# Segment attention on one core: TensorE's nine-armed lists become one list with short conditional blocks

## The chip, the cores and the metric

The kernel runs on one core of a Trainium2 chip. The metric is the device time of one execution in microseconds. The kernel before was run eight times: the median is 377.73 us, the lowest 371.74, the highest 382.41.

## The reference

Each of 16384 rows carries a segment number from 0 to 7. Each row gets a place inside its segment, at most 3072 places long, and attention runs among the rows of one segment; the result is projected, normalised over all rows, and added to the input.

```python
q = feat @ Wq; k = feat @ Wk; v = feat @ Wv            # feat 16384x256, q and k 32 wide, v 256 wide
starts = jnp.searchsorted(bids, jnp.arange(B))         # bids is not sorted here
pos = jnp.arange(N) - starts[bids]
qp, kp, vp = (pad(q), pad(k), pad(v))                  # scattered to (8, 3072, .) at [bids, pos]
scores = jnp.where(mask[:, None, :], jnp.einsum('bld,bmd->blm', qp, kp), NEG)
rp = jnp.einsum('blm,bmd->bld', jax.nn.softmax(scores, axis=-1), vp)
t = rp[bids, pos] @ Wt
tn = (t - t.mean(axis=0)) / jnp.sqrt(t.var(axis=0) + EPS) * gamma + beta
return feat + jax.nn.relu(tn)
```

Most rows fall outside the 3072 places and read an edge row, so that a segment really has some hundreds of rows of its own. A tile is 128 such rows. The kernel always handles at least four tiles of a segment and at most six.

## The kernel before, in words

**How the program is made.** The kernel is written as one list of operations in program order (`Program.op`), each with an engine, its reads and its writes. From these `settle` works out which earlier operations it must wait for; `run` then writes one instruction stream for each engine, in list order. An operation that somebody waits for raises its engine's semaphore by one. The position of a line in the source is thus its position in that engine's queue.

**The stages.** The prologue (about 0 to 30 us in the profile) finds the segments' starts, makes the list of rows of segments 0 and 1 and folds Wv and Wt into `wvt`. Then comes a loop over the eight segments, `for e in range(NB)`, here called regions 0 to 7 (about 30 to 278 us). Last, the statistics of the normalisation are finished, and sixteen groups of 1024 rows are loaded, get their edge rows added and are stored, while the segments' own rows go out by GpSimd's scatters (about 278 us to the end).

**A region.** Region e computes attention for segment e and prepares segment n = e + 1. `step(e, u)` with `attend` multiplies the probabilities of query tile u (`pa` for tiles 0 to 3, `pb` for 4 and 5) with the values `vs` of all key tiles into one of two banks `ps_o`; VectorE takes the reciprocal of the denominator (`rdens`), and the row is scaled into `tk`, on ScalarE for odd u and on VectorE for even u. Between the six steps stand, for segment n, transposes of the gathered rows (`xt_main`, `xt_rest`, copied by ScalarE into `xT`), projections (`project`), values (`values`) and scores (`scores`, with exponentials on ScalarE), and for segment e + 2 the list of rows (`own_of`, `prefix`, `list_ahead`, `list_part`, whose last act is to issue gathers on GpSimd). The banks `ps_m` are handed out in turn by `nb()`. `past` puts two VectorE sums per finished tile (`moments`) and a square on ScalarE in the gaps, and `slot` takes the next piece from the list `work` (places, edges, row numbers).

**Absent tiles.** A segment of four tiles has no products with tiles 4 and 5. Before, the whole of region e is written for TensorE nine times, once for each pair of sizes (three sizes of e by three of n); these are the arms. `sizes` computes the arm's number on VectorE, `load` (line 1070) reads it into a TensorE register, and a switch (line 776) jumps to the arm. Region 7 has three arms. Inside an arm there is no branch; at its end stands a jump over the other arms. Only TensorE has arms: the other engines do the work of six tiles always.

**Conditional blocks elsewhere.** In the last part VectorE scales tiles 4 and 5 of each segment inside `v.If(...)` (line 1902), and GpSimd scatters them inside `x.If(...)` (line 1982).

**The order of transfers.** SyncE's queue stores each segment's `tk` rows into `t_rows` (tiles 0 to 3 after step 3, tiles 4 and 5 after step 5), fetches the edge lists `eb`, and in region 7 starts to load the groups `f` (`load_group`, ten buffers, which lie partly over the attention's buffers). These loads stand in SyncE's queue behind the two stores of segment 6.

**The end.** `look` gives each engine a hint for its last branch (line 2006), by which the kernel either ends or runs the general version; TensorE's stands after its last product.

Of the kernel before, what the change touches and what calls it, by code (L numbers as in the profile page):

```python
# [20 lines left out]
P = 128  # L21
# [509 lines left out]
class Op:  # L531
    __slots__ = (
        "n", "eng", "emit", "dma", "region", "pred", "seq", "waits", "needed", "bit", "val",
        "know", "cond", "slot", "loose",
# [3 lines left out]
class Program:  # L538
# [3 lines left out]
    def __init__(self, nc):  # L542
        self.nc = nc
        self.ops = []
        self.count = {e: 0 for e in ENGINES}
        self.rings = {q: {"turn": 0, "held": [None] * n} for q, n in RINGS.items()}
        self.known = {e: ({}, 0) for e in ENGINES}
        self.records = {}
        self.where = {}
        self.region = None  # L550
        self.dmas = 0
# [35 lines left out]
    def op(self, eng, emit, reads=(), writes=(), dma=False, pred=None, cond=None, after=(), loose=False):  # L587
# [4 lines left out]
        o.needed, o.bit, o.val, o.slot = False, None, 0, None  # L592
        o.loose = loose
# [31 lines left out]
    def settle(self, o, deps):  # L625
# [42 lines left out]
        if o.region is None:  # L668
            waits, self.known[eng] = through(self.known[eng])
            o.waits = {None: waits}  # L670
            o.know = self.known[eng]
        else:
            reg = o.region
            o.waits = {}
            for arm in reg["arms"]:
                if o.pred is None or o.pred(arm):
                    o.waits[arm], reg["known"][arm] = through(reg["known"][arm])
            o.know = self.meet(list(reg["known"].values()))
        for waits in o.waits.values():
            for d in waits:  # L680
                d.needed = True
# [17 lines left out]
    def arms(self, reg, arms):  # L699
        assert self.region is None  # L700
        self.region = {"arms": list(arms), "reg": reg, "known": {a: self.known["PE"] for a in arms}}

    def end_arms(self):
        self.known["PE"] = self.meet(list(self.region["known"].values()))
        self.region = None

    def run(self):
        nc = self.nc
        sems = {e: nc.alloc_semaphore(f"at_{e}") for e in ENGINES}
        total = {e: 0 for e in ENGINES}  # L710
        for o in self.ops:
            if not o.dma:
                total[o.eng] += 1 if o.needed else 0
                o.val = total[o.eng]
        rings = {
# [13 lines left out]
        def emit(e, o, waits, inc):  # L729
            for d in waits:  # L730
# [11 lines left out]
            elif inc:  # L742
                i.then_inc(sems[o.eng], inc)

        def stream(eng):
            ops = [o for o in self.ops if o.eng == eng]

            def go(e):
                k = 0
                while k < len(ops):  # L750
                    o = ops[k]
                    if o.region is None:
                        emit(e, o, o.waits[None], 1 if o.needed else 0)
                        k += 1
                        continue
                    reg = o.region
                    end = k
                    while end < len(ops) and ops[end].region is reg:
                        end += 1
                    part = ops[k:end]  # L760
                    arms = reg["arms"]

                    def one(arm):
                        todo = []
                        for x in part:
                            if x.pred is None or x.pred(arm):
                                todo.append([x, 1 if x.needed else 0])
                            elif x.needed:
                                todo[-1][1] += 1
                        for x, inc in todo:  # L770
                            emit(e, x, x.waits[arm], inc)

                    if len(arms) == 1:
                        one(arms[0])
                    else:
                        for a in e.Switch(reg["reg"](e), len(arms)):
                            one(arms[a])
                    k = end

            return go  # L780

        for eng, e in (
            ("SP", nc.sync), ("ACT", nc.scalar), ("DVE", nc.vector), ("PE", nc.tensor), ("POOL", nc.gpsimd)
        ):
            stream(eng)(e)
# [114 lines left out]
def fast_path(nc, feat, bids, wq, wk, wv, wt, gamma, beta, out, bad):  # L900
# [86 lines left out]
    armf, arm = new("armf", [1, NB]), new("arm", [1, 2 * NB], I32)  # L987
    upto, order = new("upto", [1, NB + 1], I32), new("order", [1, NG], I32)
    tiles_i = new("tiles_i", [1, NB], I32)
# [76 lines left out]
    regs = {}  # L1066

    def load(eng, key, ap, hi, lo=0):
# [3 lines left out]
        pg.op(eng, emit, [ap], [])  # L1072
# [123 lines left out]
    def transposes(e, h, tiles, bank_, at0, which):  # L1196
        for t in tiles:
            pred = None if t < 4 or which is None else (lambda a, t=t: a[which] > t - 4)
            pg.tr(
                bank_[:, at0 + (t - tiles[0]) * P : at0 + (t - tiles[0] + 1) * P],  # L1200
                xs[:, e * FT + t, h * P : (h + 1) * P], ident[:], pred=pred,
# [5 lines left out]
    def xt_main(e, h):  # L1207
        b = nb()
        transposes(e, h, range(4), b, 0, None)
        into_xT(h, 0, QA, b[:])  # L1210

    def xt_rest(e, which):
        b = nb()
        for h in range(DH):
            transposes(e, h, range(4, 6), b, h * QB, which)
# [3 lines left out]
    def project(e, c, which, b=None):  # L1219

        b = nb() if b is None else b
        for n, pred in ((QA, None),) if c == 0 else (
            (P, lambda a: a[which] == 1), (QB, lambda a: a[which] == 2)
        ):
            for h in range(DH):
                pg.mm(
                    b[:, 0:n], w4[:, h, :], xT[:, h, c * QA : c * QA + n],
                    start=(h == 0), stop=(h == DH - 1), pred=pred,
                )
# [8 lines left out]
    def values(e, c, which):  # L1238
        b = nb()
        for i in range(2):  # L1240
            t = 2 * c + i
            pred = None if t < 4 else (lambda a, t=t: a[which] > t - 4)
            for h in range(DH):
                pg.mm(
                    b[:, i * D : (i + 1) * D], xT[:, h, t * P : (t + 1) * P], wvt[:, h, :],
                    start=(h == 0), stop=(h == DH - 1), pred=pred,
# [3 lines left out]
    def scores(e, c, tiles, which):  # L1250
        qe, ke = q[e % 2], k[e % 2]
        dst, n = (pa, QA) if c == 0 else (pb, QB)
        kinds = [(n, None)] if c == 0 else [(P, lambda a: a[which] == 1), (QB, lambda a: a[which] == 2)]
        for w, pred in kinds:
            for t in tiles:
                g = slice(32 * (t % 4), 32 * (t % 4) + 32)
                p = pred
                if t >= 4 and c == 0:
                    p = lambda a, t=t: a[which] > t - 4
                elif t == 5 and w == P:  # L1260
                    continue
                pg.mm(ps_s[t % 4][:, 0:w], ke[g, t // 4, :], qe[g, c * QA : c * QA + w], pred=p)
# [4 lines left out]
    def attend(e, u, which, between=None):  # L1267
        po = ps_o[u % 2]
        src, w = (pa, u) if u < 4 else (pb, u - 4)
        for t in (0, 1, 2, 4, 5, 3):  # L1270
            if t == 1 and between is not None:
                between()
            least = max(t, u)
            pred = None if least < 4 else (lambda a, least=least: a[which] > least - 4)
            pg.mm(
                po[:, 0 : D + 1], src[:, t, w * P : (w + 1) * P], vs[e % 2][:, t, :],
                start=(t == 0), stop=(t == 3), pred=pred,
# [3 lines left out]
        if u % 2 or e == NB - 1:  # L1281
            pg.act(tk[:, m, :], po[:, 0:D], AF.Identity, scale=rdens[:, m : m + 1])
        else:
            pg.ts(tk[:, m, :], po[:, 0:D], rdens[:, m : m + 1], ALU.mult)
        if u in (3, 5):
# [24 lines left out]
    def sizes(lo, hi):  # L1310

        n = slice(lo, hi)
        pg.ts(armf[:, n], n_bc[0:1, n], 4.0 * P, ALU.is_ge)
        pg.stt(armf[:, n], n_bc[0:1, n], 5.0 * P, armf[:, n], ALU.is_ge, ALU.add)
        pg.stt(
            arm[:, lo - 1 : hi - 1], armf[:, lo - 1 : hi - 1], 3.0, armf[:, n], ALU.mult, ALU.add,
        )

# [17 lines left out]
    list_ahead(0)  # L1336
# [709 lines left out]
```

## Time and profile before

| | |
|---|---|
| profiled execution, device time | 376.97 us |
| span of its instructions | 372.5 us |
| median of eight runs | 377.73 us |
| TensorE matmul busy | 267.8 us (72%), 1405 records |
| VectorE, ScalarE, GpSimd busy | 236.5, 149.9, 173.9 us |
| regions start on TensorE at | 30.5, 65.2, 92.3, 129.9, 169.4, 201.8, 233.7, 256.3 us |
| instruction fetches of queue q8 | 35 packets, 0.57 MB |

The span runs from the first to the last instruction; the time outside it is 4.5 us in this execution. A float32 product of 128 columns by 256 shows as two matmul records of about 0.22 us from start to start, so that one step of four key tiles has 8 records and one of six tiles has 12. From the records of the steps (8, 8, 10, 12, 12, 12, 8, 8) the segments of this input have 4, 4, 5, 6, 6, 6, 4 and 4 tiles. In the page's second part the span is cut into 40 slices of 9.3 us.

### The profile page before, as it was taken

The numbers are of one execution on the slowest core, as the hardware profiler recorded it, in microseconds if no ns is written. First come the engines' busy times: TensorE is split into PE (matmuls) and PEld (weight loads), VectorE is DVE, ScalarE is ACT, GpSimd is POOL, SyncE is SP. The second block draws the span as 40 slices with busy tenths as digits, with TensorE's granted clock in tenths as the row PEclk, the third lists the DMA queues.
The fourth block names the chain that finished last, engine by engine and source line by source line (L and its number), as shares of the span: only waits on it lengthen the run. The fifth ranks groups of instructions, "written<-read, shape, count | busy, mean of one in ns | idle before, by whom it ended". The sixth has DMA issues, their size and how long they took to land.

```text
span 372.5 us, 4981 instructions
## 1 busy us (share of the span) xinstructions
PE 267.8 (72%) x1405; PEld 177.4 (48%) x1405; DVE 236.5 (63%) x762; ACT 149.9 (40%) x291; POOL 173.9 (47%) x178
## 2 busy tenths in 40 slices
PE   5795883967789599958999897877595895454400
PEld 2563552735556377736776576645362332212100
DVE  5841687694259337722695878346457999999602
ACT  2233856835157336432663726458341131110000
POOL 6506044047726603741278457730603066887770
PEclk9567898996979879998999989898698696855555
DMA  3102013013005110410031022004998989998962
GB/s 90 49 0 60 2 40 116 4 45 101 6 15 160 23 45 24 121 37 18 6 101 35 0 54 82 16 1 154 423 398 362 418 298 425 423 421 334 349 228 114
DMA packets 22497, 52.12 MB, mean 140 GB/s; under 512 B 7503, under 2 KB 15777, under 8 KB 18475
## 3 DMA queue, kind: packets, MB, share of 16 engines
q1 hardware_dynamic: 15610, 40.85, 28.6%
q0 software_dynamic: 6288, 10.01, 8.8%
q8 instruction: 35, 0.57, 0.7%
q10 hardware_dynamic: 544, 0.52, 0.4%
q14 instruction: 20, 0.16, 0.1%
HBM read 25.37 MB, written 28.74 MB: 145 GB/s over the span
## 4 chain that ended last, share of the span: by engine, by line
PE 39%; DVE 32%; issue 12%; ACT 6%; another core or an unknown queue 6%; POOL 2%; POOLq 0%; DVEq 0%
PE ps L801 36%; DVE f L820 7%; DVE tk L820 5%; PE ps L806 3%; DVE acc L840 3%; DVE junk L827 2%; ACT pa L811 2%; DVE k L817 2%; ACT xT L811 1%; POOL sel L829 1%; DVE tk L1903 1%; DVE tk L1905 1%; DVE tk L829 1%; DVE own L840 1%
## 5 line engine op out<-in xcount | busy, mean ns | idle before, releaser
L876 POOL DMA_INDIRECT xs<-in_r_feat,idx x48 | 51.7, 1077 | 108.1 <-DVE idx L840 50.2
L801 PE MATMUL ps<-vs,pa 128*128 128x257 f32 x312 | 87.5, 433 | 17.6 <-issue 13.9
L801 PEld LDWEIGHTS ps<-vs,pa 128*128 128x128 f32 x312 | 65.4, 217 | 34.3 <-issue 18.6
L876 POOL DMA_INDIRECT reads_r<-reads_of,idx x48 | 51.3, 1069 | 14.6 <-issue 14.3
L853 DVE RECIPROCAL rdens<-ps 128x1 f32<-128x1 f32 x48 | 7.8, 162 | 67.2 <-PE ps L801 56.2
L801 PE MATMUL ps<-wvt,xT 128*128 128x256 f32 x156 | 42.9, 423 | 9.6 <-issue 4.7
L892 POOL DMA_INDIRECT out<-tk,idx x32 | 37.5, 1173 | 25.5 <-DVE f L820 14.0
L801 PEld LDWEIGHTS ps<-wvt,xT 128*128 128x128 f32 x156 | 31.5, 208 | 21.1 <-issue 8.4
L801 PE MATMUL ps<-y,hot 16*128 16x256 bf16 x384 | 20.4, 360 | 24.7 <-DVE f L820 21.1
L820 DVE TENSOR_TENSOR f<-f,ps 128x1024 f32<-128x1024 f32 (+3 forms) x17 | 26.2, 1561 | 15.8 <-remote 12.5
L816 ACT COPY f<-ps 128x1024 f32<-128x1024 f32 (+1 forms) x12 | 9.9, 834 | 62.1 <-PE ps L801 47.4
L811 ACT ACTIVATE tk<-ps,rdens 128x256 f32<-128x256 f32 x27 | 12.9, 477 | 51.8 <-DVE rdens L853 40.1
L801 PEld LDWEIGHTS ps<-y,hot 16*128 16x128 bf16 x384 | 11.1, 117 | 42.1 <-DVE f L820 30.6
L811 ACT ACTIVATE pa<-ps,mask 128x512 f32<-128x512 f32 x48 | 29.6, 693 | 3.1 <-PE ps L801 1.4
L811 ACT ACTIVATE xT<-ps,negx 128x512 f32<-128x512 f32 (+1 forms) x32 | 17.1, 586 | 31.7 <-PE ps L806 23.4
L817 DVE COPY k<-ps 32x128 f32<-32x128 f32 x48 | 14.1, 294 | 21.7 <-PE ps L801 11.2
L801 PE MATMUL ps<-f,ident 128*128 128x512 f32 x38 | 25.6, 797 | 1.8 <-DVE ecat L820 1.0
L811 ACT ACTIVATE q<-ps,cqk 96x512 f32<-96x512 f32 (+3 forms) x32 | 18.3, 573 | 17.3 <-PE ps L801 16.3
L801 PE MATMUL ps<-xT,w 128*128 128x512 f32 (+2 forms) x48 | 22.3, 592 | 2.6 <-ACT xT L811 2.6
L840 DVE SCALAR_TENSOR_TENSOR acc<-tk,reads_r,acc 128x256 f32<-128x256 f32 x45 | 21.5, 477 | 2.0 <-issue 1.9
L840 DVE SCALAR_TENSOR_TENSOR acc<-sq,reads_r,acc 128x256 f32<-128x256 f32 x45 | 21.6, 480 | 0.6 <-ACT sq L811 0.6
L801 PE MATMUL ps<-q,k 32*128 32x512 f32 (+2 forms) x124 | 20.5, 555 | 1.3 <-ACT pb L811 1.3
(262 smaller groups left out, 419.2 us busy)
## 6 DMA issues: line engine op xcount, KB each, us to landing
f<-in_r_feat SPq DMA_DIRECT2D x16, 1024.0 KB, 9.8
out<-f SPq DMA_DIRECT2D x15, 1024.0 KB, 6.1
t_rows<-tk SPq DMA_DIRECT2D x8, 512.0 KB
t_rows<-tk SPq DMA_DIRECT2D x8, 256.0 KB, 2.2
eb<-edge_of SPq DMA_DIRECT2D x64, 8.0 KB, 1.4
out<-f SPq DMA_DIRECT2D x2, 512.0 KB, 3.1
xs<-in_r_feat,idx POOLq DMA_INDIRECT x48
reads_r<-reads_of,idx POOLq DMA_INDIRECT x48
```

The costliest lines, as they stand in the source:

```text
L801: "PE", lambda e: e.matmul(out, lhsT, rhs, start=start, stop=stop, skip_group_check=True),
L806: return self.op("PE", lambda e: e.transpose(out, in_, ident), [in_, ident], [out], pred=pred)
L811: "ACT", lambda e: e.activation(out, in_, func, bias=bias, scale=scale), [in_, *more], [out]
L816: return self.op("ACT", lambda e: e.copy(out, in_), [in_], [out])
L817: return self.op(eng, lambda e: e.tensor_copy(out, in_), [in_], [out])
L820: return self.op(eng, lambda e: e.tensor_tensor(out, a, b, op), [a, b], [out])
L827: lambda e: e.tensor_scalar(out, a, s1, s2, op0, op1, accum_out=accum)
L829: else e.tensor_scalar(out, a, s1, s2, op0, op1),
L840: else e.scalar_tensor_tensor(out, a, s, b, op0, op1),
L853: return self.op("DVE", lambda e: e.reciprocal(out, in_), [in_], [out])
L876: lambda e: e.indirect_dma_start(out=out, out_offset=None, in_=table, in_offset=bass.IndirectOffsetOnAxis(ap=ind, axis=0), bounds_check=n ...
L892: lambda e: e.indirect_dma_start(out=table, out_offset=bass.IndirectOffsetOnAxis(ap=ind, axis=0), in_=src, in_offset=None, bounds_check=n ...
```

## The change

1. **No arms.** An operation may carry a condition (segment, level) instead of a function of the arm. `region_of` only keeps account of what each combination of sizes has already waited for. The streams are written once; where consecutive operations of TensorE depend on the same segment's size, they stand in one `If`, with a nested `If` for tile 5. Each segment's size is read into a register one region ahead (`size_of`). An operation inside a block raises no semaphore: its count is added to that of the next operation outside (`inc`, `due`), so whoever waits for it waits for that one. Projection and scores of columns 512 to 767 are always 256 wide; before they were 128 wide for a segment of five tiles. In region 0 a one-column product after `project(0, 1)` carries such a count.
2. **Prefix sums a step later.** `own_of(e + 3)` moves from after step 3 to after step 4, and `prefix` and `sizes` of that segment from step 4 of region e to step 0 of region e + 1, after the transposes. Segment 7's `own_of` becomes a piece of `work`.
3. **Row scaling.** The scaling of odd u is now on VectorE, right behind the reciprocal; that of even u on ScalarE, in a function `scale` of its own, which at u = 0, 2 and 4 stands behind the transposes' copies, the projection and the values. In region 7 all are on ScalarE, and steps 4 and 5 take banks from `nb()`.
4. **Fills and slots.** `fill_rows` and what is left of `work` no longer run in one go at the start of region 1; the fills become three pieces of `work`, so that the edge lists and the row numbers come later.
5. **Region 7.** `none` is set on GpSimd after region 6 (before: in region 7, behind the gather of `ecat`), and the products that open `sums` and add the row sums come after step 3 (before: step 4).
6. **TensorE leaves last.** TensorE's `look` waits for the last addition on VectorE (`added`).

```diff
@@ Program
+    def taken(o, arm):
+        return o.pred is None or arm[o.pred[0]] >= o.pred[1]
...
+                due[o.eng] += 1 if o.needed else 0
+                o.inc = 0
+                if o.pred is None and not o.bare:
+                    o.inc, due[o.eng] = due[o.eng], 0
...
-                        for a in e.Switch(reg["reg"](e), len(arms)):
-                            one(arms[a])
...
+                part = ops[k:end]
+                least = min(x.pred[1] for x in part)
+                with e.If(self.sized[seg] > least - 1):
+                    stream(e, part, least)
@@ fast_path
+    def over4(e, t):
+        return None if t < 4 else (e, t - 3)
...
-    def attend(e, u, which, between=None):
-        po = ps_o[u % 2]
+    def attend(e, u):
+        po = po_of[u] = nb() if e == NB - 1 and u >= 4 else ps_o[u % 2]
...
         pg.recip(rdens[:, m : m + 1], po[:, D : D + 1])
-        if u % 2 or e == NB - 1:
-            pg.act(tk[:, m, :], po[:, 0:D], AF.Identity, scale=rdens[:, m : m + 1])
-        else:
+        if u % 2 and e < NB - 1:
             pg.ts(tk[:, m, :], po[:, 0:D], rdens[:, m : m + 1], ALU.mult)
+
+    def scale(e, u):
+        m = e * FT + u
+        if not u % 2 or e == NB - 1:
+            pg.act(tk[:, m, :], po_of[u][:, 0:D], AF.Identity, scale=rdens[:, m : m + 1])
...
-    def step(e, u):
-        attend(e, u, 0)
+    def step(e, u, more=None):
+        attend(e, u)
+        if more is not None:
+            more()
+        scale(e, u)
...
         if e == 1:
-            fill_rows()
-            slot(99)
...
-            work.extend([*one, two, *sides, *three_])
-        if e >= 1:
-            load("PE", e, arm[0:1, e : e + 1], 8)
-        region(e, [(0,), (1,), (2,)] if last else three)
+            fills = fill_rows()
+            work.extend([fills[0], *one, fills[1], two, *sides, fills[2], *three_, lambda: own_of(NB - 1)])
+        if not last:
+            size_of(n)
+        pg.region_of((e,) if last else (e, n))
         if e == 0:
-            values(0, 1, None)
-            xt_rest(0, 0)
-            project(0, 1, 0)
-            values(0, 2, 0)
-            scores(0, 0, range(4, 6), 0)
+            xt_rest(0)
+            values(0, 1)
+            project(0, 1)
+            values(0, 2)
+            scores(0, 0, range(4, 6))
...
-            step(e, 0)
...
-            if e == 0:
-                prefix(2, 3)
-                sizes(2, 3)
+            step(e, 0, lambda: (xt_main(n, 0), xt_main(n, 1)))
+            if e + 3 < NB:
+                prefix(e + 2, e + 3)
+                sizes(e + 2)
             if busy:
                 list_ahead(e + 2)
-            xt_main(n, 0)
-            xt_main(n, 1)
...
             step(e, 3)
-            scores(n, 0, range(4), None)
-            if e + 3 < NB:
+            scores(n, 0, range(4))
+            step(e, 4, lambda: values(n, 0))
+            past(e)
+            if e + 4 < NB:
                 own_of(e + 3)
-            past(e)
...
-            step(e, 4)
-            values(n, 0, 1)
-            if e + 3 < NB:
-                prefix(e + 3, e + 4)
-                sizes(e + 3, e + 4)
...
         if e == NB - 2:
             slot(99)
+            pg.set("POOL", none[:], 0.0)
...
-            pg.tt(rows, rows, psum[:, b0 + lo : b0 + hi, :].rearrange("p b d -> p (b d)"), ALU.add)
+            added = pg.tt(rows, rows, psum[:, b0 + lo : b0 + hi, :].rearrange("p b d -> p (b d)"), ALU.add)
...
-    for eng in ("PE", "ACT", "DVE", "SP"):
+    look("PE", [added])
+    for eng in ("ACT", "DVE", "SP"):
         look(eng)
```

## The prediction

> **What bounds the kernel now.** I read the chain first, then TensorE's order of time, then the waits.
>
> ```profile
> PE 39%; DVE 32%; issue 12%; ACT 6%; another core or an unknown queue 6%; POOL 2%; POOLq 0%; DVEq 0%
> PE   5795883967789599958999897877595895454400
> DMA  3102013013005110410031022004998989998962
> ```
>
> TensorE is busy nine tenths in the middle slices (regions 2 to 5); the DMA engines are nearly idle until slice 27 and full from there on. So there are two stages: the regions, which TensorE's list and its pauses set, and a tail of 372.5 - 257.5 = 115 us from SyncE's first group load (257.53 us), which transfers set. The change works in the first; a region that ends earlier starts the loads earlier, and the tail moves with it. "Issue", 12% of the chain, is time in which an engine waited for nothing the profile shows. On TensorE it stands at the region starts:
>
> ```profile
> 28.46 1.99 PE L801 MATMUL ps<-wvt,xT 128*128 128x256 f32 x8
> 34.55 3.77 PE L801 MATMUL ps<-wvt,xT 128*128 128x256 f32 x8 [4.10 <-issue]
> ...
> 123.85 1.99 PE L801 MATMUL ps<-wvt,xT 128*128 128x256 f32 x8
> 129.88 5.41 PE L801 MATMUL ps<-vs,pa 128*128 128x257 f32 x12 [4.04 <-issue]
> ...
> 136.74 2.87 PE L801 MATMUL ps<-vs,pa 128*128 128x257 f32 x12
> ```
>
> The same product costs 5.41 us after the pause and 2.87 later: the granted clock is 0.57 in 129.8 to 136 us and 1.00 in 136 to 165. What TensorE's sequencer did is under the switch's line:
>
> ```profile
> L776 PEldq COMPARE_BRANCH  x16: 304/2892/4249, 31.0 to 270.5; - x16
> L776 PEldq COMPARE_BRANCH  x2: 3272/3657/4042, 121.4 to 125.7; - x2
> L1902 DVEq COMPARE_BRANCH  x16: 43/56/72, 296.9 to 339.6; - x16
> L1982 POOLq COMPARE_BRANCH  x16: 34/45/53, 300.7 to 347.7; - x16
> L1070 PEldq TENSOR_LOAD <-arm x8: 302/310/494, 29.7 to 252.0; - x8
> ```
>
> (Durations in ns: least, median, most. The second line is the window 120 to 131 us.) A jump into an arm takes 2 to 4 us, and in that window the instruction queue q8 shows 3 fetches. Branches over a few instructions, on VectorE and GpSimd, take about 0.05 us. The jump at 121.4 us lasted 3.27 us, yet TensorE's products ran on to 125.84: the sequencer was 4.4 us ahead.
>
> **Part by part: gains.** *Switches.* Pauses before regions 0, 1, 3, 4, 5, 6: 4.10 + 2.49 + 4.04 + 3.58 + 0.81 + 3.00 = 18.0 us; region 2 shows none, and region 7's lies under a wait for a ScalarE copy. Slow products behind them, against the same at full clock: 3.77 - 1.99, 2.59 - 1.95, 5.41 - 2.87, 4.46 - 2.87, 3.40 - 1.95, 1.33 - 1.03 = 8.3.
>
> *Prefix sums.* TensorE waits for VectorE's `own_of`:
>
> ```profile
> 58.48 0.18 PE L801 MATMUL ps<-lm,tri 128*128 128x1 bf16 x1 [2.99 <-DVE rdens L853]
> 85.27 0.18 PE L801 MATMUL ps<-lm,tri 128*128 128x1 bf16 x1 [3.69 <-DVE own L820]
> ```
>
> With 1.43 at 42.13 that is 8.1, and the slow products after the two long ones 3.28 - 1.99 + 3.78 - 1.99 = 3.1: 11.2. Half a region later nothing is late: `list_part` still has an attention step and a projection (3.9 us) ahead of it, against some 2.5 us of VectorE's prefix copies and `list_ahead`.
>
> *Row scaling.* Waits behind scaled rows in ScalarE's queue: 1.40 and 4.55 - 2.87 near 212 us, 1.26 at 245.4, 2.02 at 163.8, in all 6.4. The swap also puts rows on ScalarE, so I take half, 3.2. Segment 6's tile 5 goes to VectorE: now ScalarE writes it at 256.44, SyncE stores it at 256.97 and only then loads; VectorE has the reciprocal at 254.75 + 0.16, and 0.48 of scaling gives 255.4: 1.0 earlier.
>
> *Region 7.* TensorE waits 4.21 us for `none`. That is not ahead of the loads, but of the statistics; DMA share falls to 0.68 in 286 to 290 us while the first store waits for them, 1.3 us' worth. I take 1.0.
>
> Sum of gains 18.0 + 8.3 + 11.2 + 3.2 + 1.0 + 1.0 = 42.7.
>
> **Costs.** *Blocks.* Regions 0 to 6 have 8 blocks for e and 3 for n, region 0 three more for itself, region 7 seven: 87; each of the four segments with 5 or 6 tiles opens 10 nested ones: 127 branches. Skipping: 43 for the four segments of four tiles, 11 for segment 2: 54. No row shows a short branch on TensorE. Bounds: 127 x 0.056 = 7.1 us by VectorE's, 127 x 0.304 = 38.6 by the shortest of L776, and nothing where the 4.4 us lead covers them; less than nothing is excluded, as they only add instructions. A short block is nearest to VectorE's; where TensorE waits, in the small regions, the lead is gone. I take 5.0, range 0 to 38.6. The registers' loads (0.31 us each) remain, but a region ahead of use.
>
> [...]
>
> *Late signals.* The last blocks of a region (scores and values of tiles 4 and 5 of n) are now signalled by region n's first product. ScalarE then has two exponentials (0.63 each) and a copy (0.58), ready 0.45 + 0.1 + 1.85 = 2.4 us after the step began; the product with tile 4 is due after three others, 3 x 0.45 = 1.35. Wait 1.05 at each of four borders (into regions 2 to 5): 4.2. Bounds: 0, and 10.6 if each also brings a slow clock (1.6, as at 169.36).
>
> *VectorE in regions 0 and 1.* It is busy 18.0 of 20.5 us in 39.5 to 60, so not all of these regions' gain can be had. Its work of region 0 (from 39.05 to 63.88 with 2 us idle, less the `reads` piece and a prefix that move on) is some 20 us and could start near 33: region 1 not before 51 to 53, against 65.2. My gains there come to 13 to 14, which fits within 2 us: 2.0, bounds 0 and 8.
>
> *Small ones.* The prefix product takes a bank that ScalarE must empty first, 0.69 against a transposition of 0.5 alongside: 0.3 x 5 = 1.5. Wider products for segment 2: 10 x (0.426 - 0.321) + 0.4 = 1.4. TensorE's last branch took 6.57 us at 350.6; behind `added` (367.32) it could end at 374.0 against 372.5, with the transfers over sooner: 0.5, bounds 0 and 1.5. Together 3.4. The fills (3.0 us of ScalarE at 64.9) and edge lists move into gaps. SyncE's 16 register reads and `eb` copies come three slots later, past one store of `t_rows`, which nobody reads before region 7; VectorE's `hot` reads the copies five slots behind them, some 25 us. The `reads` table is written from region 1's first slot; the first gather of it was at 85.95, 22 us after the write. VectorE and ScalarE sat 5.96, 4.68 and 2.22 us ("remote") near 93 to 104 us, while SyncE issued those copies; I know no cause and count no gain.
>
> Costs 5.0 + 4.2 + 2.0 + 3.4 = 14.6; net 28.1. 376.97 - 28.1 = 348.9 for an execution like the profiled one, which is 0.76 under the median: **350 us**.
>
> **Rivals.** *1. New waits take the old ones' place, 362 us.* Row scaling gives nothing, the borders cost 10.6, VectorE 8: 3.2 + 6.4 + 6.0 less gain, 365; with the blocks wholly covered, 360; between. For: in regions 0 and 1 chains through VectorE end many waits. Against: regions 3 to 5 run without a gap inside their arms.
> *2. TensorE's skips go to memory, slower.* If skips cost what a jump into an arm costs (2.9 us, L776's median), 33.1 us (the net without the blocks' 5.0) are eaten by 11.4 of the 54; from there on the change is no gain, from 14 it is slower by 2%. With a third, 18: 350 - 5 + 52.2 = 397 us. For: no TensorE row below 0.30 us. Against: 32 short branches on two other engines, none over 0.072 us, and targets a few instructions away.
> *3. The tail does not move, 376 us.* The loads need buffers that hold `m3`, `w3` and segment 6's operands; were these freed as late as now, the regions' gain would end in a wait of SyncE. For: `rows` starts a slot later. Against: its last reduction ended at 250.1, 7.4 us before the loads, and VectorE is busy only 11 of 22 us in region 6.
>
> **How the numbers follow.** Chances: forecast 0.58, rival 1 0.24, rival 2 0.09, rival 3 0.09. The forecast's own terms at their good ends (blocks 0, borders 0, all 6.4 of scaling, VectorE 0) give 335, and the "remote" waits gone (12.9 at most) 323; I take 330 as the low end. The high end, 372, takes in rival 1, blocks at 0.2 us uncovered (25.4 - 5.0 = 20 more, 370) and part of rival 3. Two per cent, about what a measurement of this kernel can tell from no change, is 7.6 us. Faster: forecast, and nearly all of rival 1, 0.82; within: rival 3 and a little, 0.09; slower: rival 2, 0.09.
>
> **What would show it.** Right: TensorE's issue pauses before regions under 1 us, q8's fetches well below 35, first group load near 230 us, short branches on TensorE around 0.05 to 0.3 us. Border waits show as idle before `vs,pa`, ended by an exponential or copy of ScalarE. Wrong: compare-branches of over 2 us inside regions (rival 2), or SyncE waiting ahead of the loads for VectorE (rival 3).

## The result and the profile after: 1863 us, because a second version of the kernel ran

The changed kernel takes 1863.31 us (median of 10 runs, 1861.28 to 1869.16), the kernel before 377.60 beside it (27 runs, 370.13 to 387.59). The ratio is 4.995, with an interval of 4.979 to 5.011. The forecast was 350 us, faster.

First the page of the changed kernel: TensorE and its clock in 40 slices of 46.7 us, the instruction queue, the chain by engine and by line, and one group of instructions.

```profile
PE   7789876210000000006687577676776657638500
PEclk9889986555555555557777877678778755658855
q8 instruction: 25, 0.41, 0.1%
issue 8%; PE 8%; DVE 5%; POOL 2%; DMA 1%; ACT 0%; DVEq 0%; SPq 0%; POOLq 0%; ACTq 0%
PE ps_v L479 3%; DVE y L519 2%; DVE y L521 2%; POOL tt L491 2%; PE po L443 2%; PE ps_m L479 1%; DVE y L520 1%; PE s L421 1%; DMA t_rows<-tq 1%; PE pT L438 0%; DMA x<-x_rows 0%; DMA out<-y 0%; PE pv L403 0%; PE pqk L395 0%; PE px L391 0%
L443 PE MATMUL po<-vx,prT 128*128 x640 | 188.8, 453 | 14.7 <-ACT prT L440 14.7
```

The whole kernel as it was described stands in the first eight slices. Then comes a second program: line 443 is in `any_lengths`, the general version, of which the page of the kernel before shows no line. The lines that the chain names are also its own. So the first question is not what a region costs, but who sent the engines there. They are sent at the end of the fast part, by the value `bad`. Here is the row that writes it (duration in ns least/median/most, then first and last start):

```profile
L821 DVE TENSOR_TENSOR bad<-ps,cnt_f x1: 151/151/151, 274.1 to 274.1; 128x1 int32<-128x1 f32 x1
```

Three of the five engines' branches on it, and the timeline around them:

```profile
L2001 PEldq COMPARE_BRANCH  x1: 79/79/79, 356.3 to 356.3; - x1
L2001 SPq COMPARE_BRANCH  x1: 79/79/79, 360.2 to 360.2; - x1
L2001 POOLq COMPARE_BRANCH  x1: 48/48/48, 360.8 to 360.8; - x1
```

```profile
353.86 2.29 DVE L821 TENSOR_TENSOR f<-f,ps 128x2048 f32<-128x2048 f32 x1 [11.77 <-remote]
356.17 0.33 SPq L1915 DMA_DIRECT2D out<-f  x1
361.14 0.36 ACTq L75 DMA_DIRECT2D gamma_bc<-in_L_rec_gamma  x1
361.15 0.35 SPq L99 DMA_DIRECT2D b_i<-in_r_bids  x1
361.15 0.21 POOL masks.py:197 MEMSET ident<- 128x128 f32 x1 [9.49 <-POOLq L2003]
```

The fast part ends its additions at 356.15 us, GpSimd leaves it at 360.9, and at 361.1 the general version starts to load its own weights. The span is 1868.1 us, so 1507 us belong to the general version and 361 to the work that the forecast is about, against a span of 372.5 before.

Inside the fast part the rows that answer to those of before look as foretold. TensorE's timeline at the starts of regions 0 and 3, where it paused 4.10 and 4.04 us:

```profile
31.68 1.99 PE L802 MATMUL ps<-wvt,xT 128*128 128x256 f32 x8 [0.68 <-ACT vs L817]
...
38.92 0.18 PE L802 MATMUL ps<-lm,tri 128*128 128x1 bf16 x1 [2.39 <-ACT xT L812]
...
120.31 1.47 PE L802 MATMUL ps<-vs,pa 128*128 128x257 f32 x6
125.34 2.94 PE L802 MATMUL ps<-vs,pa 128*128 128x257 f32 x6 [3.56 <-ACT vs L817]
```

No pause for "issue" is left at either, and the products behind it run at 1.99 us again. (Two waits for "issue" of 1.24 us each stand in the first steps of regions 2 and 5; own_banks, below, has none there.) In their place stands a wait for a ScalarE copy at a border, 3.56 us where I expected 1.05. The branches of TensorE:

```profile
L779 PEldq COMPARE_BRANCH  x128: 65/65/386, 30.5 to 252.7; - x128
```

And its register loads, 8 as before, with a median of 430 ns instead of 310, a region ahead of use:

```profile
L1070 PEldq TENSOR_LOAD <-arm x8: 309/430/936, 21.7 to 221.3; - x8
```

128 short branches where 127 were counted; 73 of them take 65 to 70 ns, and 55 take 223 ns in the mean. By the forecast's count, 73 entered and 54 skipped, the short ones are the blocks entered. None takes over 0.39 us, so none shows a stop like those of the jumps into the arms, 2.2 to 4.2 us.

### The profile page after: what moved, and what is told of

Read it like the earlier page. It is cut to its first block, busy times and chain, and to the rows that moved or that the text cites. A ratio compares the mean times of both kernels' runs of the same rounds, so it can differ in the third digit from the quotient of the medians.

```text
span 1868.1 us, 14861 instructions
## 1 busy us (share of the span) xinstructions
PE 908.0 (49%) x3146; PEld 519.3 (28%) x3146; DVE 635.9 (34%) x1552; ACT 355.3 (19%) x697; POOL 440.6 (24%) x454
## 5 line engine op out<-in xcount | busy, mean ns | idle before, releaser
L297 POOL DMA_INDIRECT x_rows<-fx,oidx x128 | 124.4, 972 | 342.9 <-DMA x_rows<-fx,oidx 233.9
L443 PE MATMUL po<-vx,prT 128*128 x640 | 188.8, 453 | 14.7 <-ACT prT L440 14.7
L443 PEld LDWEIGHTS po<-vx,prT 128*128 128x128 f32 x640 | 138.3, 225 | 85.7 <-ACT prT L440 33.0
L479 PE MATMUL ps_m<-tt,ones 128*128 128x512 f32 x128 | 118.0, 1016 | 75.9 <-DMA tt<-t_rows,ridx 44.3
L421 PE MATMUL s<-kT,qw 33*128 x160 | 118.9, 856 | 64.8 <-DVE den L415 50.7
L491 POOL DMA_INDIRECT tt<-t_rows,ridx x128 | 127.7, 998 | 66.2 <-issue 66.2
L425 DVE TENSOR_REDUCE nm<-s 128x1 f32<-128x512 f32 x80 | 55.3, 691 | 79.7 <-PE s L421 79.7
L479 PEld LDWEIGHTS ps_m<-tt,ones 128*128 128x128 f32 x128 | 31.6, 288 | 161.9 <-issue 159.3
L438 PE MATMUL pT<-ident,pr 128*128 128x128 f32 x320 | 58.3, 326 | 15.5 <-ACT pr L432 15.5
L438 PEld LDWEIGHTS pT<-ident,pr 128*128 128x128 f32 x320 | 47.8, 173 | 46.6 <-ACT pr L432 39.4
L479 PE MATMUL ps_v<-sq,ones 128*128 128x512 f32 x128 | 57.2, 610 | 5.6 <-ACT sq L506 5.6
```

Source lines behind the costliest of these rows:

```text
L297: nc.gpsimd.indirect_dma_start(out=x_rows, out_offset=bass.IndirectOffsetOnAxis(ap=oidx[:, j : j + 1], axis=0), in_=fx[:, i, :], in_offset ...
L421: nc.tensor.matmul(s, qw[:, ts(t, P)], kT[:, ds(kc * CH, CH)], start=True, stop=True)
L425: nc.vector.tensor_reduce(nm, s, AX.X, ALU.max, negate=True)
L438: nc.tensor.transpose(pT[:, ts(u, P)], pr[:, ts(u, P)], ident)
L443: nc.tensor.matmul(po, prT[:, ts(u, P)], vx[:, ds(kc * CT + u, 1), :].rearrange("p x d -> p (x d)"), start=(u == 0), stop=(u == CT - 1),)
L479: nc.tensor.matmul(ps, ones, x[:, 2 * h : 2 * h + 2, :], start=(g == 0 and h == 0), stop=(g == J // GT - 1 and h == GT // 2 - 1),)
```

## The experiments

Two questions are open: what made `bad` positive, and, once it is not, whether the fast part gains the 28 us of the forecast. `bad` adds two counts: denominators that are not positive or out of bounds (`odd`), and segments that are too long (`over`).

**Theory A**: in region 7 tiles 4 and 5 take banks from `nb()`. Segment 7 has four tiles, so no product writes these banks' column 256, and the reciprocal reads what some earlier operation left there. In `ps_o` that was always an earlier denominator, which is positive; in a shared bank it can be anything. **Rival B**: a block loses a product of a tile that is present. **Rival C**: the count of long segments goes wrong since `prefix` moved.

### What sends the engines to the general version

**own_banks.**

```diff
-        po = po_of[u] = nb() if e == NB - 1 and u >= 4 else ps_o[u % 2]
+        po = po_of[u] = ps_o[u % 2]
...
+        if e == NB - 1 and u >= 4:
+            pg.mm(po[:, 511:512], ident[:], ones[:, 0:1])
         m = e * FT + u
```

> In region 7 tiles 4 and 5 take the attention banks again, as before, and a one-column product that always runs stands behind each of their blocks, since without it the row scaling of tile 4 would wait for a signal that only a later product gives. All else is as changed. Theory A (the 1500 us are the general version, entered because the denominators of two absent tiles are read from column 256 of a shared bank, which holds whatever was there last): no general version, and the time is that of the changed kernel's fast part: its span ended near 361 us where the kernel before ended at 372.5, so about 366 us against 377.7, between 361 and 371. Rival B (a product of a present tile is lost or has the wrong size in a block): still about 1863. Rival C (the count of too-long segments is read too early since the prefix sums moved): still about 1863.

Measured: 330.78 us (4 runs, 329.44 to 332.10) against 362.37 for the kernel before beside it; ratio 0.916, interval 0.909 to 0.922. No general version. Theory A stands, and the estimate of 366 was far off: 35 us too high.

**one_in_column.**

```diff
         src, w = (pa, u) if u < 4 else (pb, u - 4)
+        if e == NB - 1 and u >= 4:
+            pg.mm(po[:, D : D + 1], ident[:], ones[:, 0:1])
```

> Region 7 keeps the two shared banks for tiles 4 and 5, but a product that always runs writes 1 into column 256 of the bank ahead of each block, so that an absent tile's denominator is 1 instead of what was left there. Theory A: no general version, about 366 us (361 to 371), within 1 us of the kernel with the attention banks. Rivals B and C, which have nothing to do with the column: still about 1863.

Measured: 331.33 us, ratio 0.917 (0.911 to 0.923). With the shared banks kept and only column 256 made positive, the general version is not entered. This rules out B and C, and it names the column.

**before_shared.**

```diff
-        po = ps_o[u % 2]
+        po = nb() if e == NB - 1 and u >= 4 else ps_o[u % 2]
```

> The kernel before with nothing changed but the bank of tiles 4 and 5 in region 7, which is taken from the two shared banks. Its arms, its prefix sums and its end are untouched. Theory A: it enters the general version as the changed kernel does, about 372.5 + 1507 + some 5 around the span = 1875 to 1885 us. Rivals B and C, which lie in the blocks and the moved prefix sums: about 378 as before.

Measured: 1853.91 us, one run. Its page, TensorE in slices and the chain:

```profile
PE   7789876210000000005577587576775667778400
...
issue 8%; PE 7%; DVE 5%; POOL 2%; DMA 2%; ACT 0%; DVEq 0%; POOLq 0%; SPq 0%; ACTq 0%
```

The picture of the changed kernel, made by this one line in the kernel with arms. It lies 21 us under the low end of the estimate; the kernel before takes 16 us less in this group of runs, 362 us and not 378. What stood in the column when it was read, no run shows.

### Why the fast part gains less in some groups of runs

A group is a set of kernels run together, the kernel before always among them. own_banks was 35 us faster than the changed kernel's own fast part had let me expect. The following group, meant to tell the terms apart, brought the other extreme. The edits: old_prefix puts `own_of`, `prefix` and `sizes` back to steps 3 and 4 of the region before, on top of own_banks; old_scaling scales in `attend` again; no_branches, on top of early_signal (described below), drops or keeps each product by this input's sizes:

```diff
+        if pred is not None:
+            if (0, 0, 1, 2, 2, 2, 0, 0)[pred[0]] < pred[1]:
+                return None
+            pred = None
```

> The kernel before, unchanged, for a profile beside those of the experiments. In its first profile VectorE and ScalarE sat 13 us in all near 93 to 104 us on what the profile calls remote, and the kernel with the attention banks shows none of it. Theory D (the disturbance came with that execution, not with the kernel): about 362 us, no such waits, and region 2 some 8 to 13 us shorter than in the first profile. Rival E (it belongs to the order of the copies of the edge lists before the change, which moved): the waits are there again, 5 us or more.

> The kernel with the attention banks, with own_of, prefix and sizes put back to steps 3 and 4 of the region before. Forecast's term: 11.2 us of waits for VectorE and slow products behind them come back, 342 us against 330.8, with waits of TensorE ahead of the prefix product of 3 us in regions 0 and 1. Rival (those waits stood behind the late region starts, and lists that start earlier or elsewhere leave them covered): 331 to 334.

> The kernel with the attention banks, with the rows scaled right behind the reciprocal again, odd tiles on ScalarE, even ones on VectorE. Forecast's term: 3.2 us for the queue of ScalarE and 1.0 for the last tile of segment 6, so 335 us (331 to 338). Rival (the swap only changes which engine is late): the same within 1 us.

> The kernel with the early signals, with no branch and no register load on TensorE: the sizes of this input's segments (4, 4, 5, 6, 6, 6, 4 and 4 tiles) are written into the list, so that it leaves out what makes the kernel hold for other inputs. Forecast's term for the blocks: 5.0 us, so 323 against 328.1. Bounds: nothing, 328, if TensorE's sequencer runs ahead of its products everywhere; by the durations in the changed kernel's trace, 73 entered blocks at 0.07 us and 54 skipped ones at 0.21, 16.5 us, so 312, if nothing is covered.

Measured: before_again 377.59 us, and the kernel before 382.70 in the median of the group; old_prefix 379.71, ratio 0.998 (0.993 to 1.004); old_scaling 376.66, 0.987 (0.982 to 0.993); no_branches 370.32, 0.972 (0.961 to 0.983). As measurements of terms these failed, since their partners had run in another group, where everything was 20 to 40 us faster. before_again decided for E over D in part: waits for "remote" were there again, 9.3 us ahead of VectorE's reciprocals and 3.6 ahead of ScalarE's copy of `xT`. The page of own_banks shows none: no part of its chain (6% in before_again), and no group of instructions that waited mostly for it. But own_banks copies the same edge lists without a wait of that kind at that place, so the copies alone are not the cause.

What all kernels of this group share, the changed kernel's and the first profile of before with them, is stretches in which all engines get on slowly, here called hold-ups, at the time of GpSimd's gathers of `reads_r`: from 75 to 100 us TensorE is busy 8.45 to 12.44 of 25 us in the changed kernel and in its versions here, 18.17 and 18.84 in the two profiles of the kernel before, and 23.62 in own_banks; the changed kernel's first twelve gathers run from 76.9 to 92.3 us. Hence theory F, that these gathers hold up the engines, and rival G, that they only lie there by chance. no_reads leaves out the 48 gathers:

```diff
             m = e * FT + t
-            pg.gather(reads_r[:, m : m + 1], reads_of, idx[:, m : m + 1], N)
```

> The kernel with the early signals again, as partner of the next three. The kernel before took 362 us on the first chip of these experiments and 383 on the second, and the versions of the change 328 to 331 on the first and 370 to 380 on the second, where the trace shows all engines' small instructions held up in stretches of 77 to 93, 114 to 128 and 148 to 160 us, at the time of GpSimd's gathers of the table of reads. If the kernel before takes some 380 us here: 365 to 372. If 362: 328.

> The kernel with the early signals without the 48 gathers of reads_r (the tiles' weights in the statistics stay zero, so the mean and the variance are left out of the output). Theory F (these gathers hold up the other engines on some chips): where the kernel before takes some 380 us, about 328 against 368; where it takes 362, 326 to 329, as without them GpSimd only has less to do. Rival G (the chip holds the engines up by itself and the gathers only happen to lie there): on the slower chip 360 or more, with the stretches still there.

> The kernel before without the 48 gathers of reads_r, so that the same part is left out. Theory F: about 360 us on either kind of chip, 20 less than the kernel before on the slower, within 2 on the faster. Rival G: 375 or more on the slower.

Measured, in a group without hold-ups (kernel before 361.77): early_signal_b 328.19, no_reads 328.89, before_no_reads 366.68, ratio 1.006 (0.991 to 1.020). There the gathers cost nothing that can be measured; on the cause this group could say nothing. The last one could:

> The kernel with the attention banks in region 7 and early signals, once more. If the kernel before takes 362 us here: 328. If it takes some 380, as on the slower chip: 370 to 373, by the 370.3 of the same kernel without branches there, plus their 3.4.

> The same without the gathers of reads_r (the mean and the variance are left out of the output). If the kernel before takes 362 us here: 328.6. If some 380: theory F (the gathers hold up the engines there) 329 to 335, and the stretches in which small instructions take 0.7 us are gone; rival G (the chip does so by itself) within 4 us of the kernel with the gathers.

Measured: the kernel before 379.04; early_signal_c 360.49, ratio 0.958 (0.943 to 0.972); no_reads_c 329.11, 0.876 (0.867 to 0.886). With the gathers left out the time is that of the groups without hold-ups, 31.4 us less. For this kernel F holds and G falls; the kernel before without its gathers never ran in a group with hold-ups. early_signal_c itself lies 10 us under what I expected from no_branches, so that such groups differ among themselves. Rows of SyncE's check of a register, an instruction for which the trace shows no wait, in early_signal_b, early_signal_c and no_reads_c in turn:

```profile
L1070 SPq SEQ_ASSERT  x17: 18/18/33, 81.8 to 314.4; - x17
```

```profile
L1070 SPq SEQ_ASSERT  x17: 3/18/706, 81.4 to 353.6; - x17
```

```profile
L1070 SPq SEQ_ASSERT  x17: 18/18/33, 81.1 to 318.5; - x17
```

And what the engines did from 75 to 100 us, in the same order (busy us of PE, PEld, DVE, ACT and POOL, each with its instructions, then the granted clock, the DMA share and GB/s):

```profile
75.00:100.00 25.00, 24.16 (x126) 17.57 (x124) 18.25 (x80) 16.14 (x32) 19.40 (x19) 1.00 0.23 63
```

```profile
75.00:100.00 25.00, 12.62 (x50) 9.04 (x50) 7.16 (x35) 6.54 (x13) 12.59 (x13) 0.66 0.11 27
```

```profile
75.00:100.00 25.00, 24.10 (x127) 17.31 (x125) 18.31 (x76) 16.86 (x33) 7.08 (x6) 1.00 0.20 53
```

The first two are the same kernel: an instruction of 18 ns takes up to 706, and in 25 us TensorE, VectorE and ScalarE do about half of their work or less. In early_signal_c twelve of the gathers run from 75.8 to 91.3 us, and from 83 to 90 us TensorE is busy 0.42 of 7 us. The gathers themselves, in early_signal_c, show nothing of it, neither in their issue nor in their landing:

```profile
L877 POOL DMA_INDIRECT reads_r<-reads_of,idx x48: 992/997/1578, 75.8 to 242.7; - x48
...
DMA to landing us min/median/max: 2.2/2.2/2.2
```

In early_signal_b they took 999 ns in the median and landed after 2.4 us. The expectations speak of faster and slower chips. The runs don't bear that out: on chip 6 the kernel before took 363.20 us in one group and 379.04 in the next. Why some groups are held up and others are not stays open. So does why the hold-ups cost the mended kernel 32 us (360.49 against 328.13) and the kernel before some 17 to 20 (379 to 383 against 362).

### The forecast's terms, one by one

These are read in groups without hold-ups.

**early_signal** adds to own_banks, behind the last block of regions 0 to 6:

```diff
             scores(n, 0, range(4, 6))
             values(n, 2)
+            pg.mm(ps_o[0][:, 511:512], ident[:], ones[:, 0:1])
             past(e)
```

> As the kernel with the attention banks in region 7, and behind the last block of regions 0 to 6 a one-column product that always runs and takes the signal of the blocks' products, which otherwise the first product of the next region carries. Theory A1 (the fast part gains less than the 28 us forecast because ScalarE's copies and exponentials of tiles 4 and 5 start late at the borders: waits of 3.56, 0.96, 3.49 and 0.68 us on them in the profile): 2 to 6 us less than that kernel, about 362. Rival A2 (ScalarE is behind by its own work there, and the signal is not what it waits for): the same within 1 us, the border waits keep their size.

Measured: 328.13 us against 330.78 in the same group, 2.65 less; ratio to the kernel before 0.908 (0.903 to 0.914). The border into region 3 in own_banks and in early_signal:

```profile
103.26 1.47 PE L802 MATMUL ps<-vs,pa 128*128 128x257 f32 x6
105.69 1.57 PE L802 MATMUL ps<-vs,pa 128*128 128x257 f32 x6 [0.96 <-ACT vs L817]
```

```profile
104.35 1.57 PE L802 MATMUL ps<-vs,pa 128*128 128x257 f32 x6 [0.42 <-ACT vs L817]
```

Four such borders, 0.96 down to 0.42 each, and A1 is right at its low end. The 0.42 that is left is not ScalarE's own work at every border either: in no_branches, where every product signals for itself, TensorE's products wait for `vs` three times in all (in a group with hold-ups), in early_signal five times, four of them at these borders. early_signal is the version that beats both kernels.

**no_reads_blocks_only, no_reads_old_prefix, no_reads_old_scaling, no_reads_no_branches.** Their edits are those named above, on early_signal without the gathers; blocks_only puts back prefix sums, scaling and TensorE's last branch together.

> The kernel without the gathers of reads_r, with the prefix sums, the row scaling and TensorE's last branch as before, so that blocks with early signals stand alone for the arms (with the fills, slots and region 7's order as changed). Forecast's terms: prefix sums 11.2, scaling 3.2 and the last tile of segment 6 1.0 come back, the 0.5 of the last branch falls away: 15 us more than the kernel without the gathers, about 342. Rival (the prefix sums' waits were a consequence of the arms' pauses): 5 us or less, 333.

> The kernel with early signals and without the gathers of reads_r once more, as partner of the next three (the mean and the variance are left out of the output). If the kernel before takes 362 us here: 328.9 as before. If it takes some 380: theory F (the gathers hold up the engines) 329 to 335, rival G (the chip does so by itself) 360 or more.

> The same with own_of, prefix and sizes put back to steps 3 and 4 of the region before. All three parts put back cost 13.3 us. Forecast's term for this one: 11.2, so 340. Rival (half of it was the arms' doing, and the scaling is the larger): 4 to 6, so 334.

> The same with the rows scaled right behind the reciprocal again, odd tiles on ScalarE and even ones on VectorE. Forecast's terms: 3.2 + 1.0, so 333. By the rival above: 8, so 337.

> The same with this input's sizes written into TensorE's list, so no branch and no register load on it, and it would not hold for other inputs. Forecast's term for the blocks: 5.0, so 324. Bounds: 0 (329) if the sequencer runs ahead everywhere, 16.5 (312) if every branch of the changed kernel's trace stood uncovered.

| kernel | us | partner in its group | difference | forecast's term |
|---|---|---|---|---|
| no_reads_blocks_only | 342.23 | no_reads 328.89 | 13.3 | 15 |
| no_reads_old_prefix | 335.28 | no_reads_b 328.61 | 6.7 | 11.2 |
| no_reads_old_scaling | 338.93 | no_reads_b 328.61 | 10.3 | 3.2 + 1.0 |
| no_reads_no_branches | 325.25 | no_reads_b 328.61 | -3.4 | -5.0 |

(The intervals of the single ratios to the kernel before are 0.012 to 0.019 wide, some 4 to 7 us, so the prefix sums' 6.7 and the branches' 3.4 are no sharp figures. But the four times of a kernel never overlap with its partner's four: the closest are 326.16 and 327.27 us, for the branches.) Where the time is can be read from TensorE's waits (us in total, times, longest), over the whole span, first no_reads_b, then no_reads_old_prefix, then no_reads_old_scaling:

```profile
PE ps L802 <- ACT xT L812: 3.8, 5, 2.4
PE ps L802 <- ACT tk L812: 3.4, 3, 1.6
PE ps L802 <- ACT vs L817: 2.4, 5, 0.7
```

```profile
PE ps L802 <- DVE rdens L854: 5.2, 2, 3.0
PE ps L802 <- ACT vs L817: 3.7, 7, 0.7
```

```profile
PE ps L802 <- ACT vs L817: 10.3, 10, 2.3
```

Put the prefix sums back, and VectorE's two waits of regions 0 and 1 return, 3.0 and 2.2 us. Put the scaling back, and the waits for ScalarE's copy of `vs` grow from 2.4 to 10.3 us, some with slow products behind them: at 56.23 us four products take 2.08 us, against 1.14 for four in no_reads_b at 78.39 us. Back together they cost 13.3, less than 6.7 + 10.3 = 17.0, as if each hid part of the other.

## Why the prediction was wrong, step by step

**The step that failed** is the one on region 7. The change there has two parts, `none` with the later statistics, and the banks of steps 4 and 5. I priced the first at 1.0 us and the second not at all. It is an edit costed at nothing for which I should have named what covers it: who reads a bank that a skipped product has not written. The reciprocal does, for every tile, since only TensorE skips; and the fast part's own check looks at all 48 columns of `rdens`. It cost the 1507 us of the general version: with the attention banks, or with a 1 in the shared banks' column, the same kernel takes 331 us. None of the rivals was "the fast part is refused at its end", though the front part of this document describes the last branch and says what it decides. The cost of that outcome could be estimated as the general version's time, and the condition could be read in the code: four tiles in segment 7, which the step records show.

The bank was not a whim either. By the code (no run tried it), with an attention bank and no further product, tile 4's scaling would wait for a signal that the next product outside a block carries, and this product, of tile 2, waits for the scaling to free the bank; neither could go on. The late signals, which I priced as waits at four borders, have here the form of another bank. own_banks needs its extra product for that reason.

**The rest of the sum**, net 28.1, comes out where the engines are not held up: own_banks gains 31.6 us (362.37 - 330.78). That is partly luck. The sum was read from an execution with hold-ups, and some of its errors cancel: the scaling gives 6 us more than forecast, the prefix sums 4.5 less. The 1.0 for region 7 and the 2.0 for VectorE were not measured apart. The terms:

- *Switches.* Blocks, early signals and the rest without the reordering (no_reads_blocks_only against the kernel before, in a group where the gathers cost nothing) give a ratio of 0.938, 22.5 us of 361.77, by its interval (0.928 to 0.947) 19 to 26; the medians differ by 19.5. The sum's terms for that were 18.0 + 8.3 + 1.0 less 5.0, 2.0 and 1.4, so 18.9, at the low end.
- *Blocks.* 5.0 was a guess between 0 and 38.6; leaving the blocks out saves 3.4. Up to half of that, 4 x 0.42, may be the border waits that go with them, by an estimate from early_signal's waits, and then the branches and register loads themselves cost less still. The branches' rows add up to 17.0 us in the changed kernel, and in its trace less than 0.1 us of it falls where, by the profile's times, no product runs: TensorE's sequencer is ahead. Both kinds of row, 65 ns and 223 in the mean, are longer than VectorE's 56, from which I guessed, and the branches still cost less time than the guess.
- *Late signals.* 4.2, from waits of 1.05 at four borders; own_banks shows 0.96 at four, and the extra product wins back 2.65. The 3.56 and 7.59 us at borders of the changed kernel, in a group with hold-ups, are 0.96 in own_banks, whose regions 0 to 6 are the same.
- *Prefix sums.* 11.2 against 6.7. Of the two long waits the first returns as read, 3.0, the second as 2.2 where I had 3.69; the third, 1.43 at 42 us, has become a wait of 2.1 to 2.4 for ScalarE's copy of `xT`, in all versions of the change. I priced that bank change at 0.3.
- *Row scaling.* 4.2 against 10.3: the mis-sized term. I halved 6.4 us of waits that showed in the kernel before. Without the pauses, the old scaling makes TensorE wait 7.9 us longer for ScalarE's copies of `vs` alone (10.3 against 2.4), some of it with slow products behind (2.08 us against 1.14 for four): with the pauses gone the queue of ScalarE shows as more waits than it did, and these the swap avoids.
- *The tail.* It moves with the regions: SyncE's first group load, in before_shared (the kernel before up to region 7) and in own_banks, in the same group:

```profile
246.42 3.44 SPq L1687 DMA_DIRECT2D f<-in_r_feat  x6
```

```profile
212.18 3.67 SPq L1691 DMA_DIRECT2D f<-in_r_feat  x6
```

  34.2 us earlier, and own_banks' span ends 112.9 us after its first load, where I had 115 before. Rival 3 falls, and rival 2 with the branch rows above. (Its 2.9 us for a jump into an arm is the median of all sixteen rows; the eight jumps into arms take 2.2 to 4.2 us, 3.9 in the median, and the other eight are the jumps at the arms' ends.) Rival 1 falls with the scaling, which was to give nothing and, of the parts put back, gives the most. My argument against it was no good, though: regions 3 to 5 did have gaps inside their arms, the waits of 2.02 and 1.40 us that I had priced under the scaling. And in its own group, with hold-ups, the changed kernel's fast part, a span of 361 us against 372.5, is nearer to rival 1's time than to mine.
- *The remote waits.* I saw 12.9 us of them in the profile of before, knew no cause and counted no gain. By what no_reads_c shows they are most likely the gathers' hold-ups: its longest waits show "remote" only ahead of `f`, in the last part, 11.3 and 10.9 us. In its group, with hold-ups, early_signal_c gains 4.2% (0.943 to 0.972), about 16 us of 379, so the forecast of 28 would have been too good there by about 12.

## What to carry to other kernels

When an engine is allowed to skip work, list the readers of what it would have written, and say for each what they find there: a buffer whose stale content was harmless by its history is no longer so when it is shared. A kernel that judges its own result and has a slow way out must have that way among the rivals. And a term read from waits in a kernel that is full of pauses is a rough guide: with the pauses away, one part here was worth more than twice its term, because the queue behind the pauses showed, and another little more than half.

## What the runs showed of the hardware

- In one group of runs, 48 gathers of 128 elements of 4 bytes each, issued by GpSimd, held up the other engines: an 18 ns instruction of SyncE took up to 706 ns, and the kernel 31.4 us more (early_signal_c against no_reads_c). In another the same gathers cost nothing (328.19 us with them, 328.89 without). Beside the gathers of whole rows of 1 KB, issued by the same engine, TensorE keeps going: in early_signal_c it is busy 7.00 of 7 us from 68 to 75 us, with gathers of rows of `xs` at 73.15 and 74.52 us. Whether the small elements matter was not tried apart from the gathers themselves.
- A short conditional block on TensorE took its sequencer about 65 ns when entered and 223 in the mean when skipped, 17.0 us for 128 branches (the changed kernel; which rows are which, by the forecast's count). Leaving them out, with the register loads and the delayed signals, saved 3.4 us of 328.61 (no_reads_no_branches against no_reads_b).
